# A graph-attention layer on one core: the end of each unit in three steps, softmax exponentials in two, arguments of gathered blocks earlier

## The chip, the cores and the metric

The kernel runs on one core of a Trainium2 chip. The metric is device time in microseconds (us) of one execution, as the median of repeated runs. The engines are named as the profile names them: PE (TensorE matmul), PEld (its weight loads), DVE (VectorE), ACT (ScalarE), POOL (GpSimd), SP (SyncE, which here only issues DMAs).

## The reference

Four graph layers run one after the other on 6250 nodes and 100000 edges, each on the rectified layer norm of `x` and each added to `x`. The change touches the last one alone, a stack of three graph-attention convolutions:

```
h = x @ W;  al_s = h @ a_src;  al_d = h @ a_dst;  al_e = edge_attr @ We @ a_edge
alpha = leaky_relu(al_s[src] + al_d[dst] + al_e, 0.2)          # edges and a self loop for each node
ex    = exp(alpha - segment_max(alpha, dst)[dst])
coef  = ex / (segment_sum(ex, dst)[dst] + 1e-16)
out   = segment_sum(h[src] * coef, dst) + bias
h     = batchnorm(leaky_relu(out, 0.01)) * gamma + beta         # over all nodes
```

Edges are sorted by `dst`.

## The kernel before

`split_edges` computes one of the three convolutions. After a prologue (the products with `W`, the first group's softmax) it has one loop of 160 steps, and each convolution runs it once. The nodes are split: an early part is aggregated with one-hot matrices on PE (dense), and a late part by gathering rows and scanning them on DVE (sparse). Both are interleaved in the same loop, by an order written out by hand: on PE, DVE and ACT every instruction runs in exactly the order in which the Python code emits it (`chain` adds an order between neighbours). POOL's gathers follow an order of their own, and each is also made to wait for the last matmul that was emitted before it (`clocked`).

**The dense part.** 160 steps are 5 groups of 32 (`s` is the place in the group), and also 20 units of 8 (`u` is the place in the unit). In each step:

- PE makes `cnt` (4 windows, 8 matmul instructions, L2623 and L2624) from one-hot tiles. `cnt` has two PSUM buffers, so step k needs the copy out of `cnt` of step k-2.
- `merged(step - 1)` is that copy: ACT, L2607, `m<-cnt`, 125x1000.
- `ready(step + 2)` makes the one-hot tiles two steps ahead. ACT makes `hot_c` four times (L2436) and `hot_n` twice (L2435, 128x250 each); DVE makes `hot_n` twice (L116) and `hot_l` once (L112).
- `product(unit - 1, m)` is a generator: 50 products of the unit before (L2447, two matmul instructions each), 7 in most steps and 1 at u = 0. At u = 1 the rest is drained, and with it comes the end of the unit: `z` on ACT out of PSUM (L2450), the leaky relu on DVE (`z_w`, L121), its statistics on DVE (L2452), and the copy into `y_t` on ACT (L2454).
- `source_terms(g + 1)` takes the next group's source terms (matmuls L2357 into `x_ps`, and on DVE `one` and a reduction), in the first 20 steps of a group.
- `softmax(g + 1)` is a generator that is advanced once a step from s = 20 on. Its five exponentials with sums stand on ACT at L2390; it ends with `coef_t` (L2404, L2405), which `ready` needs from s = 30 on.

**The sparse part.** 392 gathers of 128 rows (POOL, L67, `rows<-gtable`) come in 49 blocks of `NB` = 8, in three `rows` buffers. `late()` is a generator that works through the blocks. It is advanced `pace` = 1.307 places a step, and `done` counts the places. A block has four places: the exponentials `ex` (ACT, L2502, 128x16), the multiplication `rows<-rows,ex` (DVE, 128x1040), four scan steps `acc` (DVE, L121), four more with the store to `late_hist` (two DMAs on SP, made by `bulk`). Right after the store, in the same place, `weights(c0 + NB)` puts the next block's arguments on DVE: `al` twice, the scan `top` (L2492), and `ex` three times, 128x8 each. `fetch_to` issues gathers under two conditions, one on pace and one on buffers.

In each step the order of emission is: `cnt`, at u = 1 the end of the unit, `merged`, `ready`, the products, `source_terms` and `softmax`, gathers, and then the places of `late()`.

Of the kernel before, what the change touches and what calls it, by code (L numbers as in the profile page):

```python
# [15 lines left out]
AF = mybir.ActivationFunctionType  # L16
OP = mybir.AluOpType
# [11 lines left out]
NW, NG, WCAP = 5, 10, 128  # L29
# [13 lines left out]
P1, C2, PL = 64, 392, 128  # L43
# [8 lines left out]
def kernel(ctx: ExitStack, tc: tile.TileContext, a: dict, out: bass.AP):  # L52
    nc = tc.nc
# [6 lines left out]
    def bulk(dst, src, eng=None):  # L60

        eng = eng or nc.sync
        eng.dma_start(dst[0:PS], src[0:PS])
        eng.dma_start(dst[PS:], src[PS:])
# [46 lines left out]
    def tt(o, x, y, op):  # L111
        nc.vector.tensor_tensor(o, x, y, op)  # L112
# [7 lines left out]
    def stt(o, x, s, y, op0, op1):  # L120
        nc.vector.scalar_tensor_tensor(o, x, s, y, op0=op0, op1=op1)  # L121
# [40 lines left out]
    def load_edges(pool, *names):  # L162
        for name in names:
# [16 lines left out]
                                             ap=[[C, P - 1], [1, 1]]))  # L180
# [1634 lines left out]
    W = D + 2  # L1815
# [20 lines left out]
    late_hist = dram.tile([PL * C2 + 1, W], F32, name="late_hist")  # L1836
# [433 lines left out]
    def split_edges(lt, i, first, wp, pool, ps, mv, sc):  # L2270
# [14 lines left out]
        of, al, shape = first.of, first.al, [128, NW, WCAP]  # L2285
# [78 lines left out]

        def softmax(g, al_s, of, al, wide):

            if not of:
                of = pool.tile([128, NW, WCAP], BF16, name="of")
                al = pool.tile([128, WCAP], F32, name="al_w", bufs=2)
                nc.sync.dma_start(of.rearrange("p k j -> p (k j)"), of_dram[g])  # L2370
                nc.sync.dma_start(al, ale_dram[i][g])
                wide = pool.tile([128, NW, WCAP], F32, name="wide", bufs=1)
                ts(wide, of, BIG, OP.mult, -BIG, OP.add)
            node = pool.tile([128, 2, NW], F32, name="node_w", bufs=1)
            for k in range(NW):
# [12 lines left out]
            yield  # L2388
            for k in range(NW):
                nc.scalar.activation(wide[:, k, :], wide[:, k, :], AF.Exp, bias=node[:, 0, k:k + 1], scale=1.0,  # L2390
                                     accum_out=node[:, 1, k:k + 1])
            yield
            ts(node[:, 1, :], node[:, 1, :], 1e-16, OP.add)
            nc.vector.reciprocal(node[:, 1, :], node[:, 1, :])
            ts(al, wide[:, 0, :], node[:, 1, 0:1], OP.mult)
            for k in range(1, NW):
                stt(al, wide[:, k, :], node[:, 1, k:k + 1], al, OP.mult, OP.add)
            yield
            c_ps = ps.tile([128, 128], F32, name="c_ps", tag="x_ps", bufs=2)
# [20 lines left out]
        def ready(step, half_n=None):  # L2420

            g, w0 = step // 32, step % 32 * 4
            if half_n is None:
                half_n = nodes_ready(step)
            hot_n = [pool.tile([128, 2, T * NW], of, name=f"hot_n{k}", bufs=3) for k, of in enumerate((F32, F32R))]
            hot_c = [pool.tile([128, 2, P], of, name=f"hot_c{k}", bufs=3) for k, of in enumerate((F32, F32R))]
            hot_l = pool.tile([128, 2, P], F32R, name="hot_l", bufs=3)
            hot = lt.hot[:, w0 % WB:w0 % WB + 4, :P]
            coef, high, low = coef_t[g]
            for w in range(4):  # L2430
                k, h = w % 2, w // 2
                if k == 0:
                    ts(hot_n[k][:, h, :], lt.slot[:, :T * NW], lt.id_t[:, g, w0 + w:w0 + w + 1], OP.is_equal)
                else:
                    nc.scalar.activation(hot_n[k][:, h, :], half_n[:, h, :], AF.Copy)  # L2435
                nc.scalar.activation(hot_c[k][:, h, :], hot[:, w, :], AF.Copy,  # L2436
                                     scale=(high if k else coef)[:, w0 + w:w0 + w + 1])
            tt(hot_l, hot.rearrange("p (h k) c -> p k h c", k=2)[:, 1],
               low[:, w0:w0 + 4].rearrange("p (h k) -> p k h", k=2)[:, 1, :, None].to_broadcast([128, 2, P]), OP.mult)
            return hot_n, hot_c, hot_l  # L2440

        def product(unit, m):

            g, w0 = unit // 4, unit % 4 * 32
            o = ps.tile([128, NW, 32], F32, name="o", bufs=2)
            for l in range(T):
                nc.tensor.matmul(o, lhsT=hst[:, l, :D], rhs=m[:P, l, :], start=(l == 0), stop=(l == T - 1))  # L2447
                yield
            z = pool.tile([128, NW, 32], F32, name="z_w")
            nc.scalar.activation(z, o, AF.Identity, bias=bias, scale=1.0)  # L2450
            stt(z, z, 0.01, z, OP.mult, OP.max)
            nc.vector.bn_stats(stats[:, unit, :], z.rearrange("f k q -> f (k q)"))  # L2452
            t0 = w0 // P1 * GP * NW + g * NW
            nc.scalar.activation(y_t[:, t0:t0 + NW, w0 % P1:w0 % P1 + 32], z, AF.Copy)  # L2454

        NB, given, order = 8, [], Pace(0)

# [10 lines left out]
        fetches, fetched = fetch(), 0  # L2468

        def fetch_to(pieces):  # L2470

            nonlocal fetched
            while fetched < min(C2, 2 * pieces + 16, NB * ((done - 1) // 4 + 3)):
                next(fetches)
                fetched += 1

        def late():
# [18 lines left out]
                return rows, ex, now  # L2496

            ahead = weights(0)
            for c0 in range(0, C2, NB):
                rows, ex, now = ahead  # L2500
                yield
                nc.scalar.activation(ex, ex, AF.Exp)  # L2502
                yield
                acc = pool.tile([PL, NB, W], F32, name="acc")
                tt(rows, rows, ex[:, 0, :, None].to_broadcast([PL, NB, W]), OP.mult)
                yield
                for j in range(NB):
                    if c0 + j == 0:
                        nc.vector.tensor_copy(acc[:, 0, :], rows[:, 0, :])
                    else:  # L2510
                        stt(acc[:, j, :], prev, ex[:, 1, j:j + 1], rows[:, j, :], OP.mult, OP.add)
                    prev = acc[:, j, :]
                    if j == NB // 2 - 1:
                        yield
                nc.vector.tensor_copy(acc[:, :, AL], now)
                bulk(bass.AP(tensor=late_hist.tensor, offset=late_hist.offset + c0 * W, ap=[[C2 * W, PL], [1, NB * W]]),
                     acc.rearrange("p c f -> p (c f)"))
                if c0 + NB < C2:
                    ahead = weights(c0 + NB)
            yield  # L2520
            nc.scalar.activation(tails, prev, AF.Copy)
            yield from late_fix(lt, tails, pool, ps)

# [74 lines left out]
        fetched, done = 14, 0  # L2598
# [12 lines left out]
        for step in range(steps):  # L2611
# [19 lines left out]
            if step:  # L2631
                merged(step - 1, m, counted)
            counted = cnt
            if step + 2 < steps:
                hots.append(ready(step + 2))
            for _ in islice(before, 7 if u else 1):
# [6 lines left out]
                    next(terms, None)  # L2643
                    next(soft, None)
            fetch_to((step + 1) * pace)
            while done < min(4 * (C2 // NB) + 1, (step + 1) * pace):
                next(edges_late)
                done += 1
            if done >= 4 * (C2 // NB) + 1:
                for _ in islice(edges_late, 2):  # L2650
                    done += 1
        merged(steps - 1, m, counted)
        for _ in before:
            pass
        before = product(steps // 8 - 1, m)
        for _ in edges_late:
            for _ in islice(before, 3):
# [8 lines left out]
        nc.scalar.preload_act_table_set("sqrt_and_others")  # L2666
        for _ in before:
            pass
        held = ps.tile([128, 3, D], F32, name="held", tag="x_ps", bufs=2)
        for _ in range(6):  # L2670
            nc.tensor.matmul(held, lhsT=ident[:P], rhs=hst[:, 0:3, :D], start=True, stop=True)
# [473 lines left out]
```

## Time and profile before

| | |
|---|---|
| median of 16 runs | 5339.35 us (5322.79 to 5366.77) |
| the profiled execution's own time | 5349.6 us |
| its span in the trace | 5347.2 us |
| busy in the span: PE, PEld | 4353.5 us (81%), 3091.6 us (58%) |
| busy in the span: DVE, ACT, POOL | 4046.3 us (76%), 3307.8 us (62%), 2871.6 us (54%) |
| the three loops of 160 steps | 3071 to 3746, 3830 to 4514, 4598 to 5281 us |

The three loops together are 2042 us of the span, the place of the whole change. A row of a group reads: line, engine, operation, output and inputs, shapes, count, then busy time and the mean of one in ns, then the idle time of the engine just before these instructions and what ended it. "issue" is a wait for which the profile shows no cause, "remote" one that was ended by a signal that it can't place.

### The profile page before, as it was taken

The numbers are of one execution on the slowest core, as the hardware profiler recorded it, in microseconds if no ns is written. First come the engines' busy times: TensorE is split into PE (matmuls) and PEld (weight loads), VectorE is DVE, ScalarE is ACT, GpSimd is POOL, SyncE is SP. The second block draws the span as 40 slices with busy tenths as digits, with TensorE's granted clock in tenths as the row PEclk, the third lists the DMA queues.
The fourth block names the chain that finished last, engine by engine and source line by source line (L and its number), as shares of the span: only waits on it lengthen the run. The fifth ranks groups of instructions, "written<-read, shape, count | busy, mean of one in ns | idle before, by whom it ended". The sixth has DMA issues, their size and how long they took to land.

```text
span 5347.2 us, 84662 instructions
## 1 busy us (share of the span) xinstructions
PE 4353.5 (81%) x25786; PEld 3091.6 (58%) x25786; DVE 4046.3 (76%) x12029; ACT 3307.8 (62%) x6467; POOL 2871.6 (54%) x2848
## 2 busy tenths in 40 slices
PE   1599977877888678899998888888788888788886
PEld 0245533333334345555555577877677877687776
DVE  7998858888888844667778587876777876677775
ACT  5466747777777665433354566767566666666674
POOL 1463047777777545546356266655355664465662
PEclk9999976566555679999999999999899998899998
DMA  4353255555666467788888655554444554455543
GB/s 100 96 171 114 101 174 181 179 184 186 180 180 180 134 170 239 238 247 262 257 256 268 198 139 134 140 130 115 134 128 130 139 132 110 139 134 131 134 126 104
DMA packets 577362, 868.53 MB, mean 162 GB/s; under 512 B 206555, under 2 KB 451739, under 8 KB 568450
## 3 DMA queue, kind: packets, MB, share of 16 engines
q1 hardware_dynamic: 483459, 674.15, 41.1%
q0 software_dynamic: 91104, 186.95, 14.5%
q8 instruction: 205, 3.36, 0.3%
q10 hardware_dynamic: 2332, 1.93, 0.1%
q14 instruction: 262, 2.15, 0.1%
HBM read 563.92 MB, written 298.68 MB: 161 GB/s over the span
## 4 chain that ended last, share of the span: by engine, by line
PE 27%; DVE 9%; issue 7%; ACT 5%; another core or an unknown queue 2%; DMA 1%; SPq 0%; DVEq 0%; POOL 0%; ACTq 0%
PE o L2447 11%; PE cnt L2624 8%; PE o L1544 3%; PE x_ps L2357 2%; PE cnt L2623 2%; DVE acc L121 2%; ACT m L2540 1%; ACT hot_c L2436 1%; ACT m L2607 1%; DVE hot_n L116 1%; DVE rows L112 1%; DMA hot_t<-hot_t 1%; ACT hot_n L2435 1%; DVE hot_l L112 0%
## 5 line engine op out<-in xcount | busy, mean ns | idle before, releaser
L67 POOL DMA_INDIRECT rows<-gtable,l_src x1176 | 1190.8, 1013 | 825.4 <-issue 296.0
L2447 PE MATMUL o<-m,hst 125*128 125x160 f32 x6000 | 973.8, 311 | 78.8 <-issue 77.2
L67 POOL DMA_INDIRECT rows<-table,f_src x784 | 801.4, 1022 | 368.8 <-issue 251.7
L2447 PEld LDWEIGHTS o<-m,hst 125*128 125x128 f32 x6000 | 890.0, 200 | 102.2 <-issue 101.0
L2624 PE MATMUL cnt<-hot_n,hot_c 128*125 128x250 f32 x2880 | 801.5, 374 | 145.8 <-issue 74.3
L67 POOL DMA_INDIRECT s_rows<-table,s_src x660 | 662.3, 1004 | 424.9 <-issue 177.3
L2607 ACT ACTIVATE m<-cnt 125x1000 f32<-125x1000 f32 x480 | 476.8, 993 | 335.2 <-remote 183.0
L2624 PEld LDWEIGHTS cnt<-hot_n,hot_c 128*125 128x125 f32 x2880 | 473.6, 201 | 198.4 <-issue 88.1
L1653 ACT ACTIVATE as_f<-piece 128x1000 fp32r<-128x1000 fp8e4 x390 | 381.0, 1028 | 322.6 <-issue 105.0
L923 PE MATMUL z<-w,s 128*128 128x128 f32 x1568 | 363.9, 405 | 236.4 <-DVE s L121 159.5
L923 PEld LDWEIGHTS z<-w,s 128*128 128x128 f32 x1568 | 310.5, 294 | 318.5 <-DVE s L121 197.6
L2623 PE MATMUL cnt<-hot_n,hot_l 128*125 128x250 f32 x960 | 467.6, 487 | 12.8 <-issue 10.9
L1544 PE MATMUL o<-as_f,of_two 128*128 128x500 f32 x1560 | 426.2, 418 | 36.4 <-ACT as_f L1653 18.8
L121 DVE SCALAR_TENSOR_TENSOR acc<-acc,ex,rows 128x130 f32<-128x130 f32 x1173 | 415.3, 354 | 33.8
L1407 ACT ACTIVATE adj<-cnt 128x1000 fp8e4<-128x1000 f32 x250 | 304.4, 1221 | 186.7 <-PE cnt L1406 166.2
L868 ACT ACTIVATE soft<-z 128x512 f32<-128x512 f32 x392 | 214.6, 584 | 286.6 <-remote 142.0
L2435 ACT ACTIVATE hot_n<-half_n 128x250 fp32r<-128x250 fp8e4 x960 | 386.1, 402 | 6.1 <-issue 3.0
L2436 ACT ACTIVATE hot_c<-hot,coef_t 128x125 f32<-128x125 fp8e4 x960 | 375.8, 391 | 0.1
L2436 ACT ACTIVATE hot_c<-hot,coef_h 128x125 fp32r<-128x125 fp8e4 x960 | 374.9, 390 | 0.0
L902 PE MATMUL z<-bf,w 128*128 128x512 f32 x392 | 365.4, 1032 | 8.8 <-DMA w_a<-in_L_gnn_W_agg 8.8
L116 DVE TENSOR_SCALAR hot_n<-l_slot,l_id_t 128x250 f32<-128x250 f32 x960 | 302.5, 357 | 89.1 <-remote 36.8
L1544 PEld LDWEIGHTS o<-as_f,of_two 128*128 128x128 f32 x1560 | 299.2, 195 | 119.4 <-ACT as_f L1653 26.6
(628 smaller groups left out, 8226.6 us busy)
## 6 DMA issues: line engine op xcount, KB each, us to landing
piece<-adj SPq DMA_DIRECT2D x360, 250.0 KB
late_hist<-acc SPq DMA_DIRECT2D x147, 455.0 KB
dist<-ew_dram SPq DMA_DIRECT2D x48, 1024.0 KB
sum_hist<-s_acc SPq DMA_DIRECT2D x132, 320.0 KB
adj<-adj SPq DMA_DIRECT2D x10, 3125.0 KB
hot<-hot SPq DMA_DIRECT2D x240, 128.0 KB
half_n<-node SPq DMA_DIRECT2D x480, 62.5 KB
ea<-in_edge_attr SPq DMA_DIRECT2D x54, 512.0 KB
```

The costliest lines, as they stand in the source:

```text
L67: return nc.gpsimd.indirect_dma_start(out=dst, out_offset=None, in_=table, in_offset=bass.IndirectOffsetOnAxis(ap=idx, axis=0))
L121: nc.vector.scalar_tensor_tensor(o, x, s, y, op0=op0, op1=op1)
L902: nc.tensor.matmul(z1, lhsT=w1, rhs=st["bf"][:, i % 2 * HB:(i % 2 + 1) * HB, :], start=False, stop=True)
L923: nc.tensor.matmul(z2[:, j, :], lhsT=s1[:, j, :], rhs=w2, start=False, stop=j == HB - 1)
L1544: yield nc.tensor.matmul(o[:, :n], lhsT=parts.columns(l, 1, s)[:, 0, :], rhs=adj(l), start=(l == 0 and s == 0), stop=(l == T - 1 and s == ...
L1653: nc.scalar.activation(made[-1], piece[:, at:at + n], AF.Copy)
L2435: nc.scalar.activation(hot_n[k][:, h, :], half_n[:, h, :], AF.Copy)
L2436: nc.scalar.activation(hot_c[k][:, h, :], hot[:, w, :], AF.Copy, scale=(high if k else coef)[:, w0 + w:w0 + w + 1])
L2447: nc.tensor.matmul(o, lhsT=hst[:, l, :D], rhs=m[:P, l, :], start=(l == 0), stop=(l == T - 1))
L2607: nc.scalar.activation(m[:P, :, :, u * 4:u * 4 + 4].rearrange("p l k q -> p k l q"), cnt[:P, :, :T * NW].rearrange("p w (k l) -> p k l w", ...
L2623: nc.tensor.matmul(o, lhsT=hot_l[:, h, :], rhs=hot_n[k][:, h, :], start=True, stop=False)
L2624: nc.tensor.matmul(o, lhsT=hot_c[k][:, h, :], rhs=hot_n[k][:, h, :], start=k == 0, stop=True)
```

## The change

- **End of a unit.** `product` no longer ends the unit itself; it appends a generator `unit_end` to a list. `end_some()` advances the first of the list, and is called at u = 1, 2 and 4, after `merged` and before `ready`. The three pieces are `z` (ACT); leaky relu and statistics (DVE); the copy into `y_t` (ACT).
- **Softmax.** For groups 1 to 4, the five exponentials are split in three and two by one more `yield`, so that everything behind them comes one step later.
- **hot_n.** One ACT copy of 128x500 in place of two of 128x250.
- **late().** `weights` of the next block is emitted before the scan steps of the present one, `ex` of the next block in the middle of these scan steps. Scan steps and store come one place later in the count of places. The store is one DMA in place of two.
- **fetch_to.** The lead over the pace is 20 gathers in place of 16, and a buffer is taken as free one place later, since the scan steps end one place later.

```diff
         def softmax(g, al_s, of, al, wide):
+            parted = not of
...
             for k in range(NW):
                 nc.scalar.activation(wide[:, k, :], wide[:, k, :], AF.Exp, bias=node[:, 0, k:k + 1], scale=1.0,
                                      accum_out=node[:, 1, k:k + 1])
+                if parted and k == NW // 2:
+                    yield
             yield
...
-                else:
-                    nc.scalar.activation(hot_n[k][:, h, :], half_n[:, h, :], AF.Copy)
+                elif h == 0:
+                    nc.scalar.activation(hot_n[k], half_n, AF.Copy)
...
                 yield
+            ends.append(unit_end(unit, g, w0, o))
+
+        ends = []
+
+        def unit_end(unit, g, w0, o):
+
             z = pool.tile([128, NW, 32], F32, name="z_w")
             nc.scalar.activation(z, o, AF.Identity, bias=bias, scale=1.0)
+            yield
             stt(z, z, 0.01, z, OP.mult, OP.max)
             nc.vector.bn_stats(stats[:, unit, :], z.rearrange("f k q -> f (k q)"))
+            yield
             t0 = w0 // P1 * GP * NW + g * NW
             nc.scalar.activation(y_t[:, t0:t0 + NW, w0 % P1:w0 % P1 + 32], z, AF.Copy)
+
+        def end_some():
+            if ends:
+                if next(ends[0], 0) == 0:
+                    ends.pop(0)
...
-            while fetched < min(C2, 2 * pieces + 16, NB * ((done - 1) // 4 + 3)):
+            while fetched < min(C2, 2 * pieces + 20, NB * ((done - 2) // 4 + 3)):
...
             ahead = weights(0)
+            yield
+            nc.scalar.activation(ahead[1], ahead[1], AF.Exp)
+            yield
             for c0 in range(0, C2, NB):
                 rows, ex, now = ahead
+                more = c0 + NB < C2
+                tt(rows, rows, ex[:, 0, :, None].to_broadcast([PL, NB, W]), OP.mult)
                 yield
-                nc.scalar.activation(ex, ex, AF.Exp)
+                if more:
+                    ahead = weights(c0 + NB)
                 yield
                 acc = pool.tile([PL, NB, W], F32, name="acc")
-                tt(rows, rows, ex[:, 0, :, None].to_broadcast([PL, NB, W]), OP.mult)
-                yield
                 for j in range(NB):
+                    if j == NB // 2:
+                        yield
+                        if more:
+                            nc.scalar.activation(ahead[1], ahead[1], AF.Exp)
...
-                    if j == NB // 2 - 1:
-                        yield
                 nc.vector.tensor_copy(acc[:, :, AL], now)
-                bulk(bass.AP(tensor=late_hist.tensor, ...
-                if c0 + NB < C2:
-                    ahead = weights(c0 + NB)
-            yield
+                nc.sync.dma_start(bass.AP(tensor=late_hist.tensor, ...
+                yield
...
             counted = cnt
+            if u in (1, 2, 4):
+                end_some()
             if step + 2 < steps:
                 hots.append(ready(step + 2))
...
-            while done < min(4 * (C2 // NB) + 1, (step + 1) * pace):
+            while done < min(4 * (C2 // NB) + 2, (step + 1) * pace):
...
-            if done >= 4 * (C2 // NB) + 1:
+            if done >= 4 * (C2 // NB) + 2:
...
         for _ in before:
             pass
+        while ends:
+            end_some()
```

More of the change, by code (lines that the diff above doesn't have):

```diff
@@ L2512, in late @@
                     prev = acc[:, j, :]
-                    if j == NB // 2 - 1:
-                        yield
                 nc.vector.tensor_copy(acc[:, :, AL], now)
-                bulk(bass.AP(tensor=late_hist.tensor, offset=late_hist.offset + c0 * W, ap=[[C2 * W, PL], [1, NB * W]]),
-                     acc.rearrange("p c f -> p (c f)"))
-                if c0 + NB < C2:
-                    ahead = weights(c0 + NB)
-            yield
+                nc.sync.dma_start(bass.AP(tensor=late_hist.tensor, offset=late_hist.offset + c0 * W, ap=[[C2 * W, PL], [1, NB * W]]),
+                                  acc.rearrange("p c f -> p (c f)"))
+                yield
             nc.scalar.activation(tails, prev, AF.Copy)
@@ L2668, in split_edges @@
             pass
+        while ends:
+            end_some()
         held = ps.tile([128, 3, D], F32, name="held", tag="x_ps", bufs=2)
```

## The prediction, made before the changed kernel ran

> **What bounds the kernel now.** I first read the busy times and the granted clock of the three step loops, since the change lies in them alone.
>
> ```profile
> core 0: us, PE busy (x) PEld busy (x) DVE busy (x) ACT busy (x) POOL busy (x), PEclk, DMA share, GB/s
> 3071.00:3746.00 675.00, 574.27 (x4710) 530.48 (x4711) 506.28 (x1537) 459.02 (x1255) 405.86 (x400) 0.92 0.50 131
> 3830.00:4514.00 684.00, 577.84 (x4708) 535.24 (x4709) 505.98 (x1538) 458.28 (x1255) 405.77 (x400) 0.92 0.49 129
> 4598.00:5281.00 683.00, 575.77 (x4710) 530.63 (x4711) 507.42 (x1538) 458.34 (x1256) 402.40 (x400) 0.93 0.49 127
> ```
>
> PE is busy 84 to 85% of each loop, DVE 75%, ACT 67%. A step takes 675 / 160 = 4.22 us. So PE sets the pace, and what can be won is its idle time: its rows in the list of waits add up to 103.6, 108.2 and 109.1 us, 321 us in all. There is a second loss: the granted clock is 0.92 to 0.93, because the trace grants either 1.0 or 0.5, so PE spends about 15% of the loops at half rate.
>
> Second, the groups of the three loops together: what ends PE's waits, and where ACT stands idle.
>
> ```profile
> L2624 PE MATMUL cnt<-hot_n,hot_c 128*125 128x250 f32 x2875 | 799.5, 373 | 145.8 <-issue 74.3 <-ACT m L2607 59.4 <-ACT hot_n L2435 11.2
> L2502 ACT ACTIVATE ex<-ex 128x16 f32<-128x16 f32 x147 | 31.1, 211 | 206.2 <-DVE ex L121 129.8 <-issue 31.7 <-DVE top L2492 26.7
> L2450 ACT ACTIVATE z_w<-o,l_vecs 128x160 f32<-128x160 f32 x58 | 22.4, 386 | 55.4 <-PE o L2447 24.1 <-remote 19.7 <-PE x_ps L2357 5.1
> L2454 ACT ACTIVATE y_t<-z_w 128x160 f32<-128x160 f32 x58 | 19.7, 339 | 64.3 <-DVE z_w L121 39.1 <-issue 12.2 <-DVE acc L121 6.6
> L67 POOL DMA_INDIRECT rows<-gtable,l_src x1167 | 1182.0, 1013 | 747.5 <-issue 294.5 <-PE x_ps L2357 186.9 <-remote 101.2
> ```
>
> PE waits most for `merged` (L2607), and ACT, which is not full, waits 206.2 us ahead of `ex` and 64.3 ahead of `y_t`, nearly always for DVE. How the two hang together is in the timeline, at the end of a unit inside a softmax (s = 25 and 26):
>
> ```profile
> 3944.51 0.38 ACT L2450 ACTIVATE z_w<-o,l_vecs 128x160 f32<-128x160 f32 x1
> ...
> 3946.74 0.32 DVE L121 SCALAR_TENSOR_TENSOR z_w<-z_w 128x160 f32<-128x160 f32 x1
> 3947.09 0.34 ACT L2454 ACTIVATE y_t<-z_w 128x160 f32<-128x160 f32 x1 [2.20 <-DVE z_w L121]
> ...
> 3947.33 0.99 ACT L2607 ACTIVATE m<-cnt 125x1000 f32<-125x1000 f32 x1
> ...
> 3948.37 1.00 PE L2624 MATMUL cnt<-hot_n,hot_c 128*125 128x250 f32 x2 [3.63 <-ACT m L2607]
> ```
>
> `y_t` waits 2.20 us, because DVE has scan steps and arguments queued ahead of the leaky relu; `m<-cnt` is queued behind `y_t`, and PE stands still for 3.63 us. The other form is `ex`, at s = 22:
>
> ```profile
> 4072.92 0.22 ACT L2502 ACTIVATE ex<-ex 128x16 f32<-128x16 f32 x1 [7.77 <-DVE ex L121]
> 4073.05 0.98 ACT L2607 ACTIVATE m<-cnt 125x1000 f32<-125x1000 f32 x1
> 4074.08 1.20 PE L2624 MATMUL cnt<-hot_n,hot_c 128*125 128x250 f32 x2 [4.69 <-ACT m L2607]
> ```
>
> ACT waits 7.77 us for arguments that stand at the end of a long DVE queue, with `m<-cnt` behind it again.
>
> **The change part by part.**
>
> *Waits of PE for ACT.* After the change `merged` stands ahead of `z`, the leaky relu is emitted a step later and `y_t` two steps after that; `ex` follows its arguments by two places (1.5 steps, 6.5 us) where it was one place. So the two stalls shown should go. I went through all holes of PE in the three loops, took the ACT instruction that ended last before each, and walked back on ACT to its last idle time: 34 us of the waits for `m<-cnt` lead back to an `ex` row, 31 us to a `y_t` row, 11 to `coef_h` (L2404) and 8 to the copy itself. The change removes causes of the first two, 65 us. What is late next is DVE: it makes `hot_n` and `hot_l` for the same `cnt`, and the chain of waits runs on DVE from 3930 to 3947 us, with the softmax, the scan steps and the arguments one behind the other. Ends: 0 (DVE takes over each time) and 85 (the `coef_h` and the copy's rows too). I take three quarters of 65: **-49 us**.
>
> *The clock.* After the hole of 3.63 us the first two `cnt` matmuls span 1.00 us, after that of 4.69 us 1.20, against 0.67 in an undisturbed step; the eight of a step span 2.67 against 1.56 us. The half clock lasts about 6.8 us in the trace, some two steps, of which I count one and a half: 1.7 us for each such hole. The groups show 36 waits for `m<-cnt` with 59.4 us; some 18 are long enough. 18 x 1.7 = **-30 us**. Ends: 0, and -100 if most of the 15% at half rate goes.
>
> The Trainium skill has a rule on this (TensorE: Matmul & The Clock Gate, Part 1): the clock falls to half after an idle window of about 3.4 us, and the penalty is the throttled time times one half. That agrees with 0.5 and 1.0 as the only grants in this trace. By that rule all of the throttled time, 0.075 x 2042 = 153 us, would be the prize if every hole fell under a window; it would put the sum near -200 us, and I don't take it.
>
> *hot_n in one copy.* Two copies of 402 ns become one of 128x500. The page has 128x1000 of the same types at 1028 ns (L1653), so 500 lies at about 611 on the line between: 804 - 611 = 0.19 us a step, 480 steps, 93 us of ACT's busy time. ACT is at 67% and mostly ahead, so this only shortens catching up; against it the second matmul waits 0.2 us longer for the whole tile, and PE has waited 11.2 us for that row. Ends -20 and +10; I take **-8 us**.
>
> *Gathers.* By counting through the loop, before, block 23's gathers (184 to 191) are issued in steps 65 and 66 and its arguments in step 70. After, the buffer condition opens once a block and the pace no longer holds: all eight come in step 66, and the arguments in step 69. So eight gathers have three steps, 12.7 us. One takes 0.95 us and 0.30 between them; from the end of the last to its signal the median in the trace is 1.4: 8 x 1.25 + 1.4 = 11.4 us. For 141 blocks I set, from times in the trace of before, the end of PE's work in the issuing step and of the scan steps that free the buffer, plus 11.4 us, against the time at which DVE reaches the new place of the arguments. Before, the margin is 6.0 us at the least, 10.9 in the median. After, it is 4.5 in the median, -2.9 at the least, and 15 blocks are short by 14 us in all; if a block takes 1 us longer, 23 blocks by 31 us. Behind the waiting argument on DVE are queued the scan steps, `one` and `hot_n`; `hot_n` has two steps of lead, so not all reaches PE. Ends 0 and +60; I take **+12 us**.
>
> Some gathers do last longer:
>
> ```profile
> 3511.03 1.23 DVE L112 TENSOR_TENSOR rows<-rows,ex 128x1040 f32<-128x1040 f32 x1
> 3511.15 1.93 POOL L67 DMA_INDIRECT rows<-gtable,l_src  x1 [3.68 <-PE x_ps L2357]
> 3513.39 0.94 POOL L67 DMA_INDIRECT rows<-gtable,l_src  x1 [0.30 <-issue]
> ```
>
> All 53 gathers over 1.5 us overlap this multiplication, which comes once a block, so a block is nearer to 12.4 than to 11.4 us, and that is why I take 12 and not 7. The Trainium skill speaks against a burst here (GPSIMD Engine Reference, Specifications): GpSimd shares its SBUF interfaces with VectorE, with contention when a DVE instruction has two SBUF inputs. Scan steps have two as well, but the next row in the trace after the one above ran at 1.03 us beside them. By the rule alone all eight would stretch and the gathers' term would be near the rival's 160 us.
>
> *The rest.* The split softmax moves 0.95 us of exponentials (two of five at 0.39 each, plus their sums at 0.19, overlapped) a step on; its use is counted with the first term, and `coef` comes at s = 28, two steps before `ready` needs it: 0. The store of a block is one DMA, so SP issues 147 fewer (0.43 us each in the timeline); SP waits for other engines between issues, so 0, and with no cover 63 us of SP time at most to gain. The loop's last place falls in step 150 as before: 0 for the tail.
>
> Sum: -49 - 30 - 8 + 12 = -75. The profiled execution took 5349.6 us, so 5274.6; it lies 10.2 above the median of the runs, which gives **5264 us**.
>
> **The rivals.**
>
> *DVE takes over (20%).* For it: the chain on DVE at 3930 to 3947. Against it: over the loop DVE is at 75%, and the stalls of `ex` also fall outside the softmax. A third of the first two terms: -16 - 10 - 8 + 12 = -22, a median of 5317.
>
> *Gathers late, slower (18%).* The new wait of the arguments for their block. Priced as blocks 4 us longer than 11.4 us (half of the eight gathers stretched to 1.93 us): 65 of 141 blocks short, by 160 us in all, and if DVE passes it all on, 160 - 87 = +73, a median of 5412. It decides from about 2.6 us more a block, where the shortage equals the 87 us of gains. Against it: only 53 of 1176 gathers are over 1.5 us.
>
> *More than I count (10%).* All waits that lead back to `ex` and `y_t`, those of `coef_h`, and half of the throttled time: about -65 - 11 - 75 = -151, a median of 5188.
>
> **How the numbers follow.** The forecast has 52%, with 5215 to 5310 as its own range. 0.2% is 10.7 us, about what a measurement of this kernel can tell from no change. Faster: 52 + 10 and 13 of the 20 of the second case, 75%. Same: 7, from that case's upper end. Slower: 18. The range 5190 to 5345 leaves out most of the gathers' case and half of the large gain, about 2 in 10.
>
> **What would show it.** Right: `ex` and `y_t` lose most of their 206 and 64 us of idle time; PE's waits for `m<-cnt` fall from 59 to below 20 us; the loops' clock rises to about 0.95; the loops take about 25 us less each. `al<-rows,ade`, which waited 2.3 us for DMA in all, shows some 15 to 30. Wrong: `cnt` waits for DVE `hot_n` or `hot_l` instead, or `al` waits 100 us and more for its gathers.

## The result: 4.3% slower, and the profile after

The changed kernel takes 5574.52 us, median of 11 runs (5558.12 to 5596.65), against 5345.87 us for the kernel before, median of 62 runs: a ratio of 1.0429 [1.0413, 1.0445]. The forecast was 5264. The three loops again, for the changed kernel:

```profile
core 0: us, PE busy (x) PEld busy (x) DVE busy (x) ACT busy (x) POOL busy (x), PEclk, DMA share, GB/s
3066.00:3820.50 754.50, 617.32 (x4710) 559.07 (x4710) 499.55 (x1537) 441.88 (x1096) 397.26 (x400) 0.88 0.43 117
3907.30:4665.60 758.30, 616.60 (x4710) 562.49 (x4711) 500.10 (x1538) 442.23 (x1097) 395.06 (x398) 0.88 0.43 116
4751.60:5499.80 748.20, 600.96 (x4710) 548.00 (x4711) 499.42 (x1538) 441.80 (x1097) 395.23 (x400) 0.92 0.43 116
```

The loops grew from 2042 to 2261 us, +219; the span grew by 222.5 (5347.2 to 5569.7), so the loss is here. DVE, ACT and POOL are no busier than before. PE is busy 107 us longer for the same matmuls (1728 to 1835 us), with a granted clock that fell from 0.92 to 0.88 in two of the loops, and it is idle 112 us longer (314 to 426). The groups of the three loops say where; first two rows of the kernel before, then the changed kernel:

```profile
L2357 PE MATMUL x_ps<-l_als,hot_t 128*128 128x50 bf16 x4608 | 183.1, 187 | 87.3 <-issue 77.0 <-DMA hot_t<-hot_t 8.9 <-DVE acc L121 0.5
L2447 PE MATMUL o<-m,hst 125*128 125x160 f32 x5884 | 953.7, 311 | 78.8 <-issue 77.2
```

```profile
L2357 PE MATMUL x_ps<-l_als,hot_t 128*128 128x50 bf16 x4608 | 216.3, 189 | 227.5 <-issue 226.7 <-DMA hot_t<-hot_t 0.4
L2450 PE MATMUL o<-m,hst 125*128 125x160 f32 x5884 | 982.8, 316 | 101.5 <-issue 99.2 <-DVE rows L112 1.1
L2644 PE MATMUL cnt<-hot_n,hot_c 128*125 128x250 f32 x2875 | 842.6, 388 | 80.8 <-issue 52.5 <-ACT m L2627 12.7 <-DVE hot_n L116 8.0
L2531 ACT ACTIVATE ex<-ex 128x16 f32<-128x16 f32 x144 | 29.7, 206 | 3.7 <-DVE ex L121 2.0 <-issue 1.7
L2465 ACT ACTIVATE y_t<-z_w 128x160 f32<-128x160 f32 x58 | 19.3, 332 | 4.2 <-DVE z_w L121 4.2
L112 DVE TENSOR_TENSOR al<-rows,ade 128x8 f32<-128x8 f32 x147 | 23.8, 162 | 91.8 <-DMA rows<-gtable,l_src 74.2 <-issue 17.3
```

What the forecast wanted removed is gone: `ex` waits 3.7 us where it was 206.2 (and 5.7 us at the first block of a loop, which has a line of its own), `y_t` 4.2 where it was 64.3, and PE waits 12.7 us for `m<-cnt` where it was 59.4. What came is in the row of `x_ps`. PE stands 227 us ahead of `x_ps` matmuls (87.3 before, 77.0 of it "issue") for nothing that the profile shows. Such a wait looks like this in the timeline, inside one run of products whose operands were all there:

```profile
4223.39 0.95 POOL L67 DMA_INDIRECT rows<-gtable,l_src  x1 [0.30 <-issue]
...
4224.63 0.30 PE L2450 MATMUL o<-m,hst 125*128 125x160 f32 x1 [0.18 <-issue]
4224.64 0.94 POOL L67 DMA_INDIRECT rows<-gtable,l_src  x1 [0.30 <-issue]
...
4225.35 0.54 PE L2450 MATMUL o<-m,hst 125*128 125x160 f32 x2 [0.42 <-issue]
...
4225.89 0.95 POOL L67 DMA_INDIRECT rows<-gtable,l_src  x1 [0.30 <-issue]
4226.76 0.70 PE L2450 MATMUL o<-m,hst 125*128 125x160 f32 x4 [0.87 <-issue]
4228.20 0.30 PE L2450 MATMUL o<-m,hst 125*128 125x160 f32 x1 [0.74 <-issue]
```

PE runs one, two or four matmuls and stops again, and POOL issues one gather after the other beside it. I set each moment in which PE stands between two matmuls of one product or source term against the gathers, by their starts and ends in the trace, calling gathers a run where less than 0.6 us lies between them. (Stops over 0.15 us are counted; e3_before_burst is the kernel before with its gathers bunched, described below.)

| place of the gather in its run | 1 to 3 | 4 | 5 | 6 | 7 | 8 | runs of 8 |
|---|---|---|---|---|---|---|---|
| before: share of its time in which PE stands | 0 to 2% | 3% | 5% | 14% | 16% | 22% | 46 |
| after | 0% | 1% | 9% | 25% | 36% | 41% | 137 |
| e3_before_burst | 0% | 3% | 6% | 18% | 26% | 40% | 138 |

In the 1.2 us behind a run the share is 20% before and 43% after. So PE stands late in a run of gathers, and the change tripled the runs of eight: its buffer condition opens once a block, as the prediction counted, and all eight gathers come in one step.

### The profile page after: what moved, and what is told of

It is laid out like the page before. It is cut to its first block, busy times and chain, and to the rows that moved or that the text cites. A ratio compares the mean times of both kernels' runs of the same rounds, so it can differ in the third digit from the quotient of the medians.

```text
span 5569.7 us, 83153 instructions
## 1 busy us (share of the span) xinstructions
PE 4420.1 (79%) x25786; PEld 3147.4 (57%) x25786; DVE 4022.4 (72%) x12029; ACT 3257.6 (58%) x5987; POOL 2852.0 (51%) x2848
## 4 chain that ended last, share of the span: by engine, by line
PE 33%; issue 9%; DVE 5%; ACT 3%; another core or an unknown queue 1%; DMA 1%; POOL 0%; SPq 0%; DVEq 0%; ACTq 0%
PE o L2450 13%; PE cnt L2644 9%; PE o L1544 4%; PE x_ps L2357 3%; PE cnt L2643 2%; ACT hot_c L2439 1%; DVE acc L121 1%; PE cnt L2304 1%; ACT m L2627 1%; DMA rows<-gtable,l_src 0%; DVE hot_n L116 0%; ACT m L2560 0%; ACT hot_n L2438 0%; DVE al_w L121 0%
## 5 line engine op out<-in xcount | busy, mean ns | idle before, releaser
L67 POOL DMA_INDIRECT rows<-gtable,l_src x1176 | 1167.3, 993 | 1072.2 <-PE x_ps L2357 494.1
L2450 PE MATMUL o<-m,hst 125*128 125x160 f32 x6000 | 1002.8, 316 | 101.5 <-issue 99.2
L2450 PEld LDWEIGHTS o<-m,hst 125*128 125x128 f32 x6000 | 917.7, 205 | 126.8 <-issue 125.8
L2644 PE MATMUL cnt<-hot_n,hot_c 128*125 128x250 f32 x2880 | 844.5, 388 | 80.8 <-issue 52.5
L2644 PEld LDWEIGHTS cnt<-hot_n,hot_c 128*125 128x125 f32 x2880 | 497.8, 211 | 148.7 <-issue 86.5
L923 PE MATMUL z<-w,s 128*128 128x128 f32 x1568 | 348.3, 391 | 273.8 <-DVE s L121 170.8
L2643 PE MATMUL cnt<-hot_n,hot_l 128*125 128x250 f32 x960 | 486.2, 506 | 18.2 <-issue 15.6
L923 PEld LDWEIGHTS z<-w,s 128*128 128x128 f32 x1568 | 296.0, 282 | 350.8 <-DVE s L121 204.0
L2357 PE MATMUL x_ps<-l_als,hot_t 128*128 128x50 bf16 x4608 | 216.3, 189 | 227.5 <-issue 226.7
L112 DVE TENSOR_TENSOR one<-x_ps,col 128x400 f32<-128x400 f32 x192 | 109.6, 571 | 368.5 <-remote 279.8
```

What stands on the lines that cost most here:

```text
L67: return nc.gpsimd.indirect_dma_start(out=dst, out_offset=None, in_=table, in_offset=bass.IndirectOffsetOnAxis(ap=idx, axis=0))
L923: nc.tensor.matmul(z2[:, j, :], lhsT=s1[:, j, :], rhs=w2, start=False, stop=j == HB - 1)
L2357: nc.tensor.matmul(x[:, w, :], lhsT=hot_t[:, w, :], rhs=parts[:, k, 0, :], start=(k == 0), stop=(k == 2))
L2643: nc.tensor.matmul(o, lhsT=hot_l[:, h, :], rhs=hot_n[k][:, h, :], start=True, stop=False)
L2644: nc.tensor.matmul(o, lhsT=hot_c[k][:, h, :], rhs=hot_n[k][:, h, :], start=k == 0, stop=True)
```

## The experiments

Theory: *runs* of back-to-back gathers hold PE up, and the stops bring the clock down. Rival 1, the prediction's own: the arguments come too soon for their gathers, DVE waits in `al`, and all else follows. Rival 2: one of the other parts of the change. Ratios are against the kernel before on the same chip. "Idle ahead of `x_ps`" is the row shown above, over the three loops.

The experiments ran on five chips. On three of them the kernel before takes 5339 to 5349 us, and PE stops as in the two traces above; on the other two it takes 4826 to 4827 us, and no run there showed the stops. Each of the five was seen in one batch of runs only, so it is open whether the difference belongs to the chip or to a state that it was in.

### Spread the gathers, or bunch them and keep them early

**e1_spread**: the changed kernel with a fourth `rows` buffer (paid for with the second buffer of `of`), so that the pace decides and each step issues two or three gathers.

```diff
-  rows bufs=3;  min(C2, 2 * pieces + 20, NB * ((done - 2) // 4 + 3))
+  rows bufs=4;  min(C2, 2 * pieces + 20, NB * ((done - 2) // 4 + 4))
```

> The changed kernel with a fourth rows buffer (and one buffer for the tile 'of', to make room), so that the pace alone lets the gathers go: 2 or 3 in each step where the changed kernel issues 8 in one step and none in the next two. All else as changed. Theory A (a run of back-to-back gathers holds up PE's instruction stream, seen as PE idle inside a product from the fifth gather of a run on): the idle of PE marked 'issue' falls from 394 us to about 150, and the time to 5240 to 5320. Theory B (arguments wait for their gathers, 74 us on DVE, and this is passed on to PE): the time falls as well, but PE's 'issue' idle falls only as far as the waits of al did. Theory C (the new order of late(), not the gathers): it stays at 5500 or more.

**e2_burst_early**: the same buffers, but a lead of 40, so that the buffer condition decides again: eight at once, with six to seven steps to spare before the arguments.

```diff
-  2 * pieces + 20
+  2 * pieces + 40          # on top of e1_spread
```

> The changed kernel with four rows buffers, but a lead so long that the buffers alone hold the gathers: 8 in one step as in the changed kernel, six or seven steps ahead of their arguments where it was three or four. Theory A (runs of gathers): still 5540 to 5600, PE's 'issue' idle still 350 us and more, while the waits of al for DMA are gone. Theory B (late arguments): 5260 to 5350.

**e3_before_burst**: the kernel before with nothing changed but its lead, 28 for 16, which makes it issue eight at once too.

```diff
-  2 * pieces + 16
+  2 * pieces + 28          # in the kernel before
```

> The kernel before with one edit, a lead of 28 gathers in place of 16: 8 gathers in one step, five or six steps ahead of their arguments. Units, softmax, hot_n and late() as before. Theory A: slower by 120 to 230 us, with PE's 'issue' idle up by 100 us and more. Theory B and theory C: within 20 us of before.

Measured: spread 0.9888 [0.9852, 0.9925]; early burst 1.0507 [1.0464, 1.055]; the kernel before with bursts 1.04 [1.035, 1.0449]. From the groups of e2_burst_early, and then a row of e3_before_burst:

```profile
L2357 PE MATMUL x_ps<-l_als,hot_t 128*128 128x50 bf16 x4608 | 220.7, 189 | 238.4 <-issue 237.2 <-DMA hot_t<-hot_t 0.7
L112 DVE TENSOR_TENSOR al<-rows,ade 128x8 f32<-128x8 f32 x147 | 23.6, 161 | 4.1 <-DMA rows<-gtable,l_src 2.9 <-issue 0.8
```

```profile
L2357 PE MATMUL x_ps<-l_als,hot_t 128*128 128x50 bf16 x4608 | 202.3, 189 | 169.5 <-issue 161.5 <-DMA hot_t<-hot_t 3.2 <-DVE ex L121 1.2
```

In e2_burst_early `al` waits 2.9 us for its rows in place of 74.2, and the kernel is slower still. So the lateness that I had priced is there in the changed kernel, but its removal wins nothing; rival 1 falls. In e3_before_burst nothing of the change is present but the bunching, its `ex` still waits 194.1 us, the idle ahead of `x_ps` rises from 87.3 to 169.5, and it loses nearly what the change lost; so rival 2 can hold little of the loss. That the changed kernel has 227 us there, and this one 169.5, is a difference that no run explains: beside bursts the other parts of the change win nothing.

### The other parts alone

**e4_units_alone**: the kernel before with the ends of units in three steps, the split softmax and the single `hot_n` copy; gathers and `late()` as before.

```diff
+  unit_end / end_some, softmax's third yield, hot_n in one copy     # late(), weights(), fetch_to unchanged
```

> The kernel before with the ends of units in three steps, the softmax exponentials in two and hot_n in one copy; late() and the gathers as before. By the prediction's terms this keeps the half of the waits that leads back to y_t (31 us of the 65), about half of the clock's term and the 8 us of hot_n: faster by 30 to 60 us. If DVE takes over: faster by less than 20.

Measured: 0.9986 [0.9965, 1.0007], no difference, where 30 to 60 us were expected. Two groups:

```profile
L2465 ACT ACTIVATE y_t<-z_w 128x160 f32<-128x160 f32 x58 | 19.2, 331 | 4.4 <-DVE z_w L121 2.6 <-DVE sc L121 1.8
L2518 ACT ACTIVATE ex<-ex 128x16 f32<-128x16 f32 x147 | 31.2, 212 | 225.1 <-DVE ex L121 126.6 <-DVE top L2508 49.9 <-issue 22.1
```

`y_t` no longer waits, but `ex` waits 225 us in place of 206: ACT comes to `ex` sooner and stands there instead. PE's waits for `m<-cnt` fell only from 59.4 to 39.6 us, and these 20 us came back as "issue" ahead of `o`, 77.2 to 95.7. The two causes of these waits are in a row on one engine, so taking away one hands part of its share to the other.

### Can the gathers be issued better?

**e5_even**: e1_spread with the gathers issued at three points of a step. **e6_fours** and **e18_fours_again**: e1_spread with gathers in fours.

```diff
+  fetch_to((step + 0.33) * pace); ... fetch_to((step + 0.67) * pace)          # e5_even, e11_even
+  2 + 4 * int((2 * pieces + 20) // 4)  in place of  2 * pieces + 20           # e6_fours, e18_fours_again
```

> As e1_spread, but the gathers of a step are issued at three points of it (after cnt, after four of the seven products, at the end) and so wait for three different matmuls: mostly one at a time. Theory A1 (what counts is how many gathers follow each other without a pause): nearly no runs over 4, PE's idle inside products and source terms falls from e1's 160 us to under 80, the time to 5180 to 5250. Theory A2 (what counts is how many gathers fall into some 10 us, pauses or not): as e1_spread within 15 us.

> As e1_spread, but gathers are let go four at a time: four in one step, then none until the next four are due, about 6.5 us later. Theory A1 (a run holds PE up from its fifth gather on, and a pause of over 1 us ends it): few runs over 4, PE's idle inside products and source terms under 80 us, 5180 to 5250. If the fifth is not the threshold, but every busy stretch of POOL adds: as e1_spread, 5260 to 5300.

**e7_no_gathers**: one DMA of fixed rows for each block from SP, in place of its eight gathers. **e8_half_rows**: e2_burst_early with gathers of 64 rows and a memset on DVE for the other 64.

```diff
-  order.gather(given[-1][:, c % NB, :], table, lt.src[:, c:c + 1])
+  if c % NB == 0: nc.sync.dma_start(given[-1], <fixed rows of table>)          # e7_no_gathers, e10_no_gathers
+  if c % NB == 0: nc.vector.memset(given[-1][64:], 0.0)                        # e8_half_rows, e16_half_again
+  order.gather(given[-1][:64, c % NB, :], table, lt.src[:64, c:c + 1])
```

> As e2_burst_early (four buffers, a block at a time, early), but the 8 gathers of a block are replaced by one DMA on SP that loads 8 x 128 rows of 520 bytes from fixed places, with the same wait for PE (it leaves out the indices, so the rows are others). The same bytes in the same pieces arrive in the same bursts, and POOL issues nothing in the loops. Theory P (the gathers' work on POOL and its software queue hold PE up): PE's 'issue' idle falls from 450 us to under 100, the time to 5130 to 5230. Theory D (the traffic of the bursts holds it up): it stays above 5450.

> As e2_burst_early, but each gather brings 64 rows in place of 128 (the other half is set to zero on DVE once a block, 49 instructions a loop more; it leaves out the edges of 64 partitions). Theory A by time: the run is as long as POOL works on it. If a gather of 64 rows takes POOL half as long, runs last 6 us instead of 10 and PE's mid-product idle falls to a third or less, 5250 to 5350; if it takes as long as before, runs stay 10 us and the time stays at 5560 to 5620. Theory D (traffic): half the traffic, so about half of the loss, near 5450, whatever POOL's time.

These four fell on a chip without stops: 0.9816 [0.98, 0.9833], 0.9824 [0.9803, 0.9845], 0.9725 [0.9706, 0.9745] and 1.0108 [1.0088, 1.0128]. PE did not stand inside products in any of them, so they said nothing on the theory. The last is slower with its memsets on DVE, which is busy 539 of 590 us there; PE waits 40.1 us for DVE's `hot_n` (11.6 in e6_fours) and 56.3 for DMAs of `hot_t` (8.0). Whether its bursts cost something besides was not told apart.

So four were run together, and now on a chip with stops:

> The changed kernel once more, to stand on the same chip as the three runs beside it. If the chip shows TensorE standing in the middle of products while gathers run back to back (before at some 5340 us on it), 1.043 times the kernel before, with some 220 us or more of such idle ahead of x_ps in the loops. If the chip is one where before takes some 4830 us and TensorE does not stand there, the theory that the loss is those stalls and the clock that follows them gives 0.975 to 0.99, as the evenly issued version had 0.982 there; the rival, that a burst of eight gathers costs by itself on every chip (the waits of al for its rows, or something else of the burst), gives 1.00 to 1.04.

> Version with a fourth rows buffer in which one plain DMA for each block, of fixed rows, stands in the place of its eight gathers (the values of the rows are therefore others). Theory: it is the gathers on GpSimd that hold TensorE up; without them the idle ahead of x_ps falls under 60 us in the loops and the time is 0.96 to 0.975 of before on either chip. Rival: TensorE stands for a reason of its own (its instruction supply against any traffic of the queues); then the idle ahead of x_ps stays over 150 us where the chip shows it, and the time is 1.02 to 1.05.

> The spread version with the issues of gathers at three points of a step, one or so at each. Theory of runs: no run of gathers passes three, so TensorE does not stand, and the time is at or below that of the spread version beside it (0.975 to 0.989). Rival, that two or three in a row were harmless already: the same time as the spread version within 0.3%.

> The spread version (fourth rows buffer, two or three gathers a step) again, for the comparison with the three beside it: 0.989 of before where the chip shows the stalls, 0.98 to 0.985 where before takes some 4830 us. If the changed kernel loses on a chip without stalls, this one still has to gain there.

Measured: the changed kernel 1.0418 [1.0396, 1.044], without gathers 0.9258 [0.9235, 0.9281] (faster than the 0.96 to 0.975 expected), even 0.9869 [0.9847, 0.9891], spread 0.9851 [0.9826, 0.9876]. The row ahead of `x_ps`, for spread and then for no gathers:

```profile
L2357 PE MATMUL x_ps<-l_als,hot_t 128*128 128x50 bf16 x4608 | 178.0, 186 | 66.7 <-issue 63.4 <-DVE acc L121 1.2 <-DVE top L2508 1.1
```

```profile
L2357 PE MATMUL x_ps<-l_als,hot_t 128*128 128x50 bf16 x4608 | 158.2, 185 | 22.4 <-DMA hot_t<-hot_t 22.0 <-DVE z_w L121 0.3
```

Without these gathers the "issue" wait ahead of `x_ps` is gone. Some 29.0 us of it are left ahead of `o` and 10.5 ahead of `cnt`, and they make the case stronger: all of them lie in the last 25 us of each loop, where GpSimd works through 20 other gathers in a row, `agg<-late_hist`. In the first loop, with the first and the ninth of these gathers:

```profile
3576.22 0.96 POOL L67 DMA_INDIRECT agg<-late_hist,l_end  x1 [1.67 <-DMA late_hist<-fixed,l_fix]
...
3586.23 0.94 POOL L67 DMA_INDIRECT agg<-late_hist,l_end  x1 [0.30 <-issue]
3586.88 0.27 PE L2645 MATMUL cnt<-hot_n,hot_c 128*125 128x250 f32 x1 [0.84 <-issue]
3587.48 1.28 POOL L67 DMA_INDIRECT agg<-late_hist,l_end  x1 [0.30 <-issue]
3588.29 0.37 PE L2645 MATMUL cnt<-hot_n,hot_c 128*125 128x250 f32 x1 [1.14 <-issue]
```

From there PE stands 13.3 of 17.7 us. Here the stops begin some 9 to 10 us into the run (in all three loops), later than beside the gathers of `rows`.

Without the gathers of `rows` a loop takes 551 us where it is 757 in the changed kernel and 648 in the spread version on the same chip. So the gathers are the cause, and spreading them saves about half of what they cost (109 of 206 us a loop): runs of five and more still form (317 of 1176 gathers stand at the fifth place or later, against 591 in the changed kernel). Issuing at three points a step changed nothing more. POOL can fall behind and then works off what is queued, so an even order in the code is not an even order on the engine.

### What of a gather is it?

**e13_burst_again** repeats e2_burst_early as the control; **e14_pool_busy** has memsets on GpSimd in place of gathers, **e15_plain_eight** plain DMAs from GpSimd's queue, **e16_half_again** half the rows.

```diff
+  order.follow(nc.gpsimd.memset(busy, 0.0))                                    # e14_pool_busy, 128x900, beside the DMA of e7
+  order.follow(nc.gpsimd.dma_start(given[-1][:, c % NB, :], <fixed rows>))     # e15_plain_eight
```

> The version with eight gathers at once and a fourth rows buffer again, as the control for the three beside it, which differ from it in the gathers alone. Where the chip shows the stalls: 1.045 to 1.055 of before and 220 to 240 us of idle ahead of x_ps in the loops. On a chip without them: about 0.98 to 1.00, and the idle ahead of x_ps under 40 us.

> One plain DMA of fixed rows for each block in the place of its gathers (the rows are therefore others), and in the place of each gather a memset of 900 elements on GpSimd, about 1 us by the 0.22 us of the one of 128 elements; three rows buffers. Theory A, it is the descriptors or transfers of the gathers that hold TensorE up: idle ahead of x_ps under 40 us and 0.925 to 0.94 of before, as without gathers. Theory B, it is GpSimd running back to back as such (its instruction stream, or the memory port beside VectorE): the idle ahead of x_ps comes back to over 100 us and the time to 0.98 or more.

> Eight plain DMAs of fixed rows for each block on GpSimd's queue, 128 rows of 520 bytes each, in the place of the eight gathers (the rows are therefore others). Theory A1, any transfer whose descriptors GpSimd writes holds TensorE up: idle ahead of x_ps 150 to 240 us, time 1.02 to 1.05. Theory A2, it is the indexed form alone: under 60 us and 0.925 to 0.96.

> Gathers of 64 rows in the place of 128, eight at once as in the control; the other half of the rows buffer is filled by a memset on VectorE, 147 times 0.93 us. If it is the number of rows or descriptors that holds TensorE up, the idle ahead of x_ps falls to 60 us or less, at a time of 0.96 to 1.00 with the memsets in it; if each gather costs the same whatever its rows, 200 us or more stay and the time is 1.05 to 1.08.

Measured: 1.0521 [1.0485, 1.0557], 0.9643 [0.9625, 0.9662], 0.9255 [0.9237, 0.9273] and 1.0573 [1.0551, 1.0594]. POOL's and PE's rows of e14_pool_busy:

```profile
L2484 POOL MEMSET busy<- 128x900 f32 x1165 | 1007.2, 865 | 729.8 <-PE x_ps L2357 382.7 <-PE o L2450 227.6 <-PE at_ps L2574 28.5
L2357 PE MATMUL x_ps<-l_als,hot_t 128*128 128x50 bf16 x4608 | 159.5, 185 | 83.1 <-DMA hot_t<-hot_t 68.7 <-DVE acc L121 9.9 <-DVE one L112 4.5
```

Of e16_half_again:

```profile
L67 POOL DMA_INDIRECT rows<-gtable,l_src x1167 | 1119.1, 959 | 1068.3 <-PE x_ps L2357 525.6 <-issue 323.9 <-PE o L2450 93.2
L2357 PE MATMUL x_ps<-l_als,hot_t 128*128 128x50 bf16 x4608 | 223.0, 192 | 237.1 <-issue 235.4 <-DMA hot_t<-hot_t 0.9
```

- GpSimd busy as such doesn't hold PE up: with memsets the idle ahead of `x_ps` has no "issue" in it, though eight of them run 7.4 us on end, longer than the four gathers and a part of the fifth (5 to 6 us) after which the stops begin. (This version was expected at 0.925 to 0.94 and is slower; DVE is busy 567 us a loop, where it was 488 with neither gathers nor memsets, and PE waits for DMAs of `hot_t`, with three `rows` buffers in place of four. I did not tell these apart.)
- The number of rows doesn't matter: 64 rows take GpSimd 959 ns where 128 took 996 in e2_burst_early, and PE stands just as long.
- Eight plain transfers issued by GpSimd cost PE nothing that shows (idle ahead of `x_ps` 16.2 us, no "issue"; row below). But they are shorter, eight in 4.2 us by the timeline, and such a run ends before the time of the fifth gather. So these runs don't tell whether it is the indexed form or a long run of any transfers that GpSimd issues.

```profile
L2357 PE MATMUL x_ps<-l_als,hot_t 128*128 128x50 bf16 x4608 | 156.1, 184 | 16.2 <-DVE one L112 10.5 <-DMA hot_t<-hot_t 5.4
```

In e14_pool_busy and e15_plain_eight too, the only "issue" stops of PE in the loops are those beside the `agg` gathers at the end.

### Where the change wins

**e17_before_spread**: the kernel before with a fourth `rows` buffer and nothing else of the change; **e18_fours_again** beside it.

```diff
-  rows bufs=3;  min(C2, 2 * pieces + 16, NB * ((done - 1) // 4 + 3))
+  rows bufs=4;  min(C2, 2 * pieces + 16, NB * ((done - 1) // 4 + 4))           # in the kernel before
```

> The kernel before with a fourth rows buffer and nothing else of the change, so that it issues two or three gathers a step where it issues up to six now. If the gain of the spread version is all in the spreading of the gathers: 0.98 to 0.99 of before, with the waits of ex and y_t as before (about 200 and 60 us). If the other parts of the change (ends of units, exponentials one place on) are worth what the spread version shows: 0.995 to 1.00 here. Where the chip shows no stalls, 0.995 to 1.005 by both.

> The spread version with its gathers issued four at a time, in every second step or so. The share of time in which TensorE stands rose from the fifth gather of a run on, so four at a time should cost nothing against two or three a step: 0.98 to 0.99 of before, idle ahead of x_ps in the loops 50 to 80 us. If the number in an issue rather than in a run counts, 1.00 to 1.02 and over 120 us of that idle.

On a chip without stops: 0.9986 [0.9974, 0.9998] and 0.9819 [0.9794, 0.9844]. Both have a fourth buffer and neither issues eight gathers at once, so nearly all of the change's intended effect lies between them. First e17_before_spread, then e18_fours_again:

```profile
L2624 PE MATMUL cnt<-hot_n,hot_c 128*125 128x250 f32 x2880 | 759.2, 361 | 114.1 <-ACT m L2607 109.6 <-ACT hot_n L2435 3.7 <-issue 0.3
L2502 ACT ACTIVATE ex<-ex 128x16 f32<-128x16 f32 x147 | 31.3, 213 | 205.0 <-DVE ex L121 203.9 <-DVE ex L112 1.2
```

```profile
L2644 PE MATMUL cnt<-hot_n,hot_c 128*125 128x250 f32 x2877 | 739.4, 354 | 33.6 <-ACT m L2627 18.5 <-DVE hot_n L116 10.8 <-ACT hot_n L2438 2.4
L2531 ACT ACTIVATE ex<-ex 128x16 f32<-128x16 f32 x144 | 29.6, 206 | 27.3 <-DVE ex L121 26.8 <-DVE ex L112 0.3
```

PE's waits for `m<-cnt` fall by 91 us and the loops from 575.5, 573.2, 574.7 to 545.6, 543.6, 545.2 us: 89 us in all, 84 in the medians (4819.23 to 4735.36). The changed kernel as it stands was not run on such a chip, so whether it gains there is open.

## Why the prediction was wrong, step by step

- **What bounds the kernel.** PE's idle time was read rightly as the thing to win. But 77.0 us of it ahead of `x_ps`, 77.2 ahead of `o` and 74.3 ahead of `cnt` were "issue", against 59.4 for `m<-cnt`: that PE waits most for `merged` is not what the row shown there says. The prediction has no term for these waits. They were the largest in the loops, 239 us in all, and the change made them larger.
- **Waits of PE for ACT, -49.** Right in mechanism: 59.4 to 12.7 us, -47, and not by the bunching, as e3_before_burst still has 57.3. Its shares (34, 31, 11 and 8) add up to 84, more than the 66 us of all PE's waits that the profile puts down to ACT, so the near hit is in part luck. Where nothing else stops PE, e18_fours_again against e17_before_spread shows 91 us, and the time shows 84 of them. The unit ends alone were worth nothing (e4_units_alone), as `ex` took their share over.
- **The clock, -30.** Wrong sign. 1 minus the granted clock, taken twice and times each loop, gives some 310 us at half rate before and 480 after. I counted only holes for `m<-cnt`, and the stops beside gathers are holes too: without gathers the clock of the loops is 0.97 to 0.98. Nor were 18 of the 36 holes long: the 18th longest is 0.88 us. The Trainium skill's measure of the penalty (TensorE: Matmul & The Clock Gate, Part 1), the throttled time times one half, would by estimate make 85 us of the 170 more; PE's busy time rose by 107, and the other 22 are open. How stops of under 1 us bring the clock down is in the trace of the changed kernel. Its half-rate stretches last 3.41 us or multiples of that, so the loops can be cut into stretches of 3.41 us. Of those at full rate 93 are followed by half rate; in each of these PE stands 1.2 to 3.0 us in all (2.28 in the median), and in 37 of them no single stop reaches 1 us. In those followed by full rate it stands 1.6 us at most. So the stops add up, and one idle window of some 3.4 us, the rule that the prediction weighed, is not needed.
- **hot_n in one copy, -8.** 611 ns, as worked out.
- **Gathers, +12.** This is the step that failed. Its count was right (eight in one step, three steps of lead) and `al` waits 74.2 us for rows, above the 15 to 30 given for right. But it priced a burst only as rows that land late on DVE. What a burst costs is PE standing beside it: the loops lost 219 us with all gains already in that figure, where the ends were 0 and +60, and without these gathers a loop takes 551 us in place of 757. Neither sign of being wrong that it named came (8.0 us for `hot_n`; 74.2, not 100, for the gathers). The Trainium skill's contention rule that I weighed (GPSIMD Engine Reference, Specifications) was about GpSimd and VectorE; the cost is not there, as DVE is busy 500 us a loop where it was 507, and e2_burst_early shows the loss with 2.9 us of waits for rows.
- **The rest, 0.** Nothing contradicts it.
- **The rivals.** *Gathers late* had the right sign and the right place by luck: a third of the size (+73 for +229) and the wrong mechanism. *DVE takes over* did not come: `cnt` waits 8.0 us for `hot_n`. *More than I count*, -151, did not come either: on a chip without stops the gain of e18_fours_again, 84 to 91 us, is near the forecast's 75.

Of the versions that leave nothing out, the best on a chip with stops is e12_spread_again, at 0.9851 of before (e11_even's 0.9869 is within its interval); its kind, in fours, is at 0.9819 on one without.

## What to carry to other kernels

A wait that the profile puts down to "issue" can have a cause that an edit moves; before an edit moves other engines' work, set these waits against what runs beside them, because the edit may multiply it. Several short stops can cost clock as one long one does. Where gathers are issued under a buffer condition and a pace, the one that binds decides whether they come in bursts, and one more buffer can be worth more than a later need. Two waits in a row on one engine are best removed together; here the second took over part of what the first gave.

## What the hardware showed that was not expected

Gathers that run back to back on GpSimd make PE stop in the middle of products whose operands are ready: from about 5 us into a run on, 41% of the time at the eighth gather and 43% just behind it. Beside the 20 `agg` gathers it is 13.3 of 17.7 us, from some 9 to 10 us into the run on. That was so on three of the five chips. In e5_even, on a chip without stops, GpSimd worked through one run of 392 gathers, a whole loop's, and PE never stood inside a product. Without gathers a loop takes 551 us on the one kind of chip (e10_no_gathers) and 534 on the other (e7_no_gathers, the same kernel), where the evenly issued version takes 656 (e11_even) and 545 (e5_even, the same kernel): most of the difference between the kinds is this. Half as many rows in a gather save neither PE's time nor much of GpSimd's (959 for 996 ns).

Stops that each last under 1 us bring the clock down together. In the loops of all twenty traces, every stretch of 3.41 us at full rate in which PE stood for more than 2.0 us in all was followed by half rate, and none in which it stood for less than 0.9 us was.

Why a run of gathers reaches PE is not settled. The transfers of the queue that the profile marks "instruction" are no slower: the 38 of 16 KB in the first loop take 0.96 us before and 0.98 after in the median, and 1.04 in e5_even, where PE doesn't stop.
